# A pass's activations in two halves of two tiles, with ScalarE's two copies of the transposes put before and behind the second activation

## The chip, the cores and the metric

The kernel runs on one core of one Trainium2 chip. The metric is the device time of one execution in microseconds (us), taken as the median of the runs. The engines are named as the profile names them: PE is TensorE's matmul side (PEld its weight loads), ACT is ScalarE, DVE is VectorE, POOL is GpSimd, SP is SyncE, which here only issues DMAs.

## The reference

The computation is one layer of a graph network on 12,500 nodes with 256 channels, all in float32. It normalises x, adds a graph convolution over 200,000 sorted edges and a linear attention, and then a feed-forward part of 30 iterations. The change is in the last one:

```python
def step(h, _):
    h = h + 0.01 * jnp.tanh(h)
    h = h * jax.nn.sigmoid(h)
    h = _layernorm(h, ln_w, ln_b)
    h = jnp.einsum('bsc,dc->bsd', h, W) + b
    return (h, None)
x, _ = jax.lax.scan(step, x, None, length=N_ITERS)     # N_ITERS = 30
```

In front of it stand `x = x + gnn(...) + mix(...)` and a layer norm; behind it the result is added to x.

## The kernel before

**Tiles and groups.** The 12,500 nodes are 98 tiles of 128 rows (the last one partly filled). Four tiles make a group: 24 groups of four tiles and one group of two. A *pass* is one iteration of the feed-forward for one group, so there are 25 x 30 = 750 passes, 720 of them of four tiles.

**Two parts.** Up to about 480 us the kernel normalises x, makes the transposed copies and the attention's matrices, and begins the edge sums. After that one loop (L1083) runs over the *steps* that a planner (`plan`) wrote down beforehand. A step holds at most one item: a pass of a group, or a product for a group's base ("mix" for the attention, "W" for the graph convolution). Up to five groups are under way at a time, and the same group comes again after four steps at the earliest, usually five. Beside the items a step can hold edge work ("octets"): gathers on POOL, selections on DVE (L213, L218, L226), edge matmuls on PE (L239, L261), a copy on ACT (L250 or L275) and a memset on DVE (L276).

**One pass, over several steps.** If a pass is the item of step k:

- Step k, PE: eight transposes of the normed tiles z into two PSUM tiles `pt`, two tiles of nodes each (L1057; four transposes per `pt`). ACT copies each `pt` into its half of `zT` (L1064, two copies of 128x512).
- Step k+1, PE: the product with the weight matrix, 16 matmul instructions (L1070), into a PSUM tile `po` of 128x1024. There are two `po` and two `pt` buffers.
- Step k+2, ACT: `s = tanh(po)` (L1016). DVE: `s = 0.01*s + po` (L1022, called the sum here; it is also the last reader of `po`). ACT: `s = silu(s)` (L1023). DVE: the statistics of s (L1029, two instructions). POOL: the variance and its power -1/2 (L1033, L1035).
- One or two steps later, DVE: z from s and the statistics (L1043, four instructions), and then the transposes of the group's next pass.

So in one step k three passes are at work: the transposes and copies of the pass of step k, the product of the pass of step k-1, and the activations of the pass of step k-2. Every engine takes its instructions in the order in which the loop writes them:

- PE: transposes(k), product(k-1), edge matmuls;
- ACT: edge copy, tanh(k-2), copy 0 (k), copy 1 (k), silu(k-2);
- DVE: selections, memset, sum(k-2), z for the items of the next two steps, statistics(k-2).

The transposes of step k+1 write the same two `pt` buffers that the copies of step k read: the first four wait for copy 0, the last four for copy 1, and product(k), which reads `zT`, stands behind them on PE.

A group's first pass has its own entry ("fresh", L1149 to L1207): statistics of the base, a scaling on ACT and DVE (L1174, L1178), and the same tanh, sum and silu, called from the same functions `act1` and `act2`.

Of the kernel before, what the change touches and what calls it, by code (L numbers as in the profile page):

```python
# [10 lines left out]
AF = mybir.ActivationFunctionType  # L11
ALU = mybir.AluOpType
# [19 lines left out]
def gps_layer(  # L32
# [22 lines left out]
    nc = tc.nc  # L55
# [25 lines left out]
    def rows_io(ap, tl, t0, nt, load, eng):  # L81
        full = nt if (t0 + nt) * P <= N else nt - 1
        parts = []
        if full:
            parts.append((tl[:, :full, :], ap[t0 * P : (t0 + full) * P, :].rearrange("(g p) c -> p g c", p=P)))
        if full < nt:
            parts.append((tl[:TAIL, full, :], ap[(t0 + full) * P : N, :]))
        for s, d in parts:
            if load:
                eng.dma_start(out=s, in_=d)  # L90
            else:
                eng.dma_start(out=d, in_=s)
# [533 lines left out]
    with tc.If(n_out > 0):  # L626
        with ExitStack() as pg_:
# [12 lines left out]
            for t in range(NE):  # L640
# [34 lines left out]
                    op1=ALU.mult, accum_out=cnt[:rows],  # L675
# [22 lines left out]
            for gi, (t0, nt) in enumerate(groups):  # L698
                ac = gp.tile([P, G, C], F32, name="ac", bufs=1)
                load_rows(acc, ac, t0, nt, nc.sync)  # L700
                for j in range(nt):
                    pt = p_t.tile([P, KC, P], F32, name="pt")
# [304 lines left out]

    def flat(h, nt):  # L1010
        return h[:, : nt // 2].rearrange("p q c j -> p (q c j)")

    def act1(gi, h):
        nt = groups[gi][1]
        s = hp.tile([P, G // 2, C, 2], F32, name="s")
        nc.scalar.activation(flat(s, nt), flat(h, nt), AF.Tanh)  # L1016
        return s

    def act2(gi, h, s):
        nt = groups[gi][1]  # L1020
        sf = flat(s, nt)
        nc.vector.scalar_tensor_tensor(sf, sf, 0.01, flat(h, nt), op0=ALU.mult, op1=ALU.add)  # L1022
        nc.scalar.activation(sf, sf, AF.Silu)  # L1023

    def stats(gi, s):
        t0, nt = groups[gi]
# [31 lines left out]
            pts.append(pt)  # L1058
        zTs[gi] = (zT, pts)

    def copies(gi):
        zT, pts = zTs[gi]
        for q, pt in enumerate(pts):
            nc.scalar.activation(zT[:, 2 * q : 2 * q + 2], pt, AF.Copy, bias=1.0)  # L1064

    def matrix(nt, lhsT, rhs, paired=False):
# [16 lines left out]
    for k in range(K + 3):  # L1083
# [5 lines left out]
        kind, gi = item(k)[:2]  # L1089
        if kind in ("mix", "W"):  # L1090
            t0, nt = groups[gi]
# [25 lines left out]
        last = kind2 == "pass" and item(k - 2)[2] == FFN_ITERS - 1  # L1117
        if kind2 == "pass" and not last:
            s2 = act1(g2, pos[kind2, g2])
        if kind == "pass":  # L1120
            copies(gi)
        if kind2 == "pass" and not last:
            act2(g2, pos.pop((kind2, g2)), s2)
        elif last:
            t0, nt = groups[g2]
            for q in range(nt // 2):
                h = pos[kind2, g2][:, q].rearrange("p c j -> p j c")
                r = slice(2 * q, 2 * q + 2)
                nc.vector.tensor_tensor(base[g2][:, r, :], h, base[g2][:, r, :], ALU.add)  # L1129
            pos.pop((kind2, g2))  # L1130
            rows_io(out, base[g2], t0, nt, False, nc.sync)
            written[g2] = k
        elif kind2 == "mix":
            nt = groups[g2][1]
            nc.vector.tensor_tensor(base[g2], pos.pop((kind2, g2))[:, :nt, :], xts.pop((kind2, g2))[:, :nt, :], ALU.add)
            if g2 < ed.weighted:
                aT = ed.aT.pop(g2).rearrange("p k (g n) -> p k g n", n=P)
                for i in range(KC):
                    bk = base[g2][:, :, i * P : (i + 1) * P]
                    nc.vector.scalar_tensor_tensor(bk, aT[:, i], 0.0, bk, op0=ALU.max, op1=ALU.add)  # L1140
        elif kind2 == "W":
            nt = groups[g2][1]
            ac = xts.pop((kind2, g2))[:, :nt, :]
            nc.vector.tensor_tensor(ac, pos.pop((kind2, g2))[:, :nt, :], ac, ALU.add)
            nc.vector.scalar_tensor_tensor(base[g2], ac, 0.0, base[g2], op0=ALU.max, op1=ALU.add)
# [3 lines left out]
        for g3, k3 in fresh:  # L1149
            if k == k3 + 4:  # L1150
                act2(g3, *first_norm[g3])
# [4 lines left out]
        for g3, k3 in fresh:  # L1156
            nt = groups[g3][1]
            if k in (k3 + 2, k3 + 3):
                mv, rs = first_norm[g3, "stats"]
                if k == k3 + 2:  # L1160

                    if 0 in written and written[0] + 2 <= k:
                        h = base[0].rearrange("p g c -> p (g c)").rearrange("p (q c j) -> p q c j", c=C, j=2)
                    else:
                        h = fp.tile([P, G // 2, C, 2], F32, name="z", bufs=3)
                    sh = fp.tile([P, G], F32, name="f_ve")
                    nc.vector.scalar_tensor_tensor(
                        sh[:, :nt], mv[:, :nt, 0], -1.0, rs[:, :nt], op0=ALU.mult, op1=ALU.mult
                    )
                    first_norm[g3, "h"] = (h, sh)  # L1170
                h, sh = first_norm[g3, "h"]
                q = k - k3 - 2
                if 2 * q < nt:
                    nc.scalar.activation(  # L1174
                        h[:, q, :, 0], base[g3][:, 2 * q, :], AF.Identity, bias=sh[:, 2 * q : 2 * q + 1],
                        scale=rs[:, 2 * q : 2 * q + 1],
                    )
                    nc.vector.tensor_scalar(  # L1178
                        h[:, q, :, 1], base[g3][:, 2 * q + 1, :], mv[:, 2 * q + 1, 0:1], rs[:, 2 * q + 1 : 2 * q + 2],
                        ALU.subtract, ALU.mult,  # L1180
                    )
                if k == k3 + 3:
                    first_norm[g3] = (h, act1(g3, h))
# [5 lines left out]
        for g3, k3 in list(fresh):  # L1189
            nt = groups[g3][1]  # L1190
# [48 lines left out]
```

## Time and profile before

| what | value |
|---|---|
| runs of the kernel | 4190.81 us median of 3 (4182.11 to 4192.11) |
| the profiled execution's own time | 4187.49 us |
| its span in the trace | 4185.7 us (1.8 us lie around it) |
| granted clock of TensorE | 0.991 of full speed over the span, 1.00 from 480 us on |
| busy share of the span, PE / DVE / ACT / POOL | 97% / 81% / 60% / 62% |
| loop from 480 to 4186 us: PE / DVE / ACT busy | 3655.6 / 3121.8 / 2344.3 of 3706 us |

How to read it: a row of the profile's groups names the line, the engine and the operation, what is written and read, the shape and the count, then the busy time in us, the mean of one in ns, and after the second bar the time for which the engine stood idle just before such instructions, with what ended it. A row of the timeline gives the start and the length in us, the engine, the line, the operation, the count of instructions merged into the row, and in brackets the idle time of the engine before the row. A busy share is a mean over stages; the end of a matmul is modelled, so that PE's spacing from start to start tells more than its busy time.

### The profile page before, as it was taken

The numbers are of one execution on the slowest core, as the hardware profiler recorded it, in microseconds if no ns is written. First come the engines' busy times: TensorE is split into PE (matmuls) and PEld (weight loads), VectorE is DVE, ScalarE is ACT, GpSimd is POOL, SyncE is SP. The second block draws the span as 40 slices with busy tenths as digits, with TensorE's granted clock in tenths as the row PEclk, the third lists the DMA queues.
The fourth block names the chain that finished last, engine by engine and source line by source line (L and its number), as shares of the span: only waits on it lengthen the run. The fifth ranks groups of instructions, "written<-read, shape, count | busy, mean of one in ns | idle before, by whom it ended". The sixth has DMA issues, their size and how long they took to land.

```text
span 4185.7 us, 67249 instructions
## 1 busy us (share of the span) xinstructions
PE 4057.6 (97%) x23817; PEld 3358.3 (80%) x23817; DVE 3401.4 (81%) x7400; ACT 2523.0 (60%) x3762; POOL 2577.9 (62%) x3189
## 2 busy tenths in 40 slices
PE   8897899999999999999999999999999999999999
PEld 5444678888888888888888888888888888888888
DVE  8554568888888888888888888888888888888887
ACT  7331246666666666666666666666656666667775
POOL 3564666777777777777777777777667652222222
PEclk9898999999999999999999999999999999999999
DMA  8332532222222222222222222222222210000000
GB/s 262 108 87 72 147 98 66 65 61 65 75 61 72 76 64 74 73 66 71 72 65 72 77 65 72 70 74 61 72 70 59 65 50 14 6 6 1 1 1 23
DMA packets 147685, 278.31 MB, mean 66 GB/s; under 512 B 28048, under 2 KB 97198, under 8 KB 147342
## 3 DMA queue, kind: packets, MB, share of 16 engines
q0 software_dynamic: 75024, 204.97, 17.0%
q1 hardware_dynamic: 72173, 68.42, 5.4%
q8 instruction: 194, 3.18, 0.3%
q14 instruction: 150, 1.22, 0.1%
q10 hardware_dynamic: 144, 0.52, 0.0%
HBM read 247.68 MB, written 26.12 MB: 65 GB/s over the span
## 4 chain that ended last, share of the span: by engine, by line
PE 77%; DVE 11%; ACT 3%; issue 3%; POOL 2%; another core or an unknown queue 1%; POOLq 0%; DVEq 0%; ACTq 0%
PE po L1070 53%; PE pt L1057 13%; PE pq L239 4%; DVE z L1043 4%; PE pkv L290 3%; PE pa L261 3%; DVE st L1029 2%; DVE s L1022 2%; ACT s L1016 2%; POOL rs L1035 1%; PE pacc L316 1%; ACT s L1023 1%; POOL xg L187 0%; DVE big L1129 0%
## 5 line engine op out<-in xcount | busy, mean ns | idle before, releaser
L1070 PE MATMUL po<-w,zT 128*128 128x256 f32 x11760 | 2669.8, 380 | 4.8 <-ACT zT L1064 2.3
L1070 PEld LDWEIGHTS po<-w,zT 128*128 128x128 f32 x11760 | 2178.4, 190 | 285.2 <-issue 7.8
L187 POOL DMA_INDIRECT xg<-xnd,src_i x1563 | 1597.4, 1022 | 512.9 <-issue 308.6
L1023 ACT ACTIVATE s<-s 128x1024 f32<-128x1024 f32 (+1 forms) x750 | 780.5, 1041 | 598.5 <-DVE s L1022 584.9
L1043 DVE TENSOR_SCALAR z<-s,st,rs 128x256 f32<-128x256 f32 x2940 | 1031.5, 418 | 100.7 <-POOL rs L1035 96.0
L1029 DVE BATCH_NORM_STATS2 st<-s 128x6 f32<-128x512 f32 x1470 | 938.7, 680 | 181.6 <-ACT s L1023 163.8
L1022 DVE SCALAR_TENSOR_TENSOR s<-s,po 128x1024 f32<-128x1024 f32 x725 | 864.3, 1192 | 251.4 <-ACT s L1016 181.3
L1016 ACT ACTIVATE s<-po 128x1024 f32<-128x1024 f32 x725 | 729.6, 1006 | 209.0 <-PE po L1070 197.6
L1064 ACT ACTIVATE zT<-pt 128x512 f32<-128x512 f32 x1470 | 801.5, 602 | 61.2 <-PE pt L1057 55.0
L1057 PE MATMUL pt<-ident,z 128*128 128x128 f32 x5880 | 792.7, 276 | 38.9 <-DVE z L1043 37.5
L1057 PEld LDWEIGHTS pt<-ident,z 128*128 128x128 f32 x5880 | 670.1, 141 | 182.6 <-issue 81.6
L1035 POOL TENSOR_TENSOR rs<-ve,mhalf 128x4 f32<-128x4 f32 (+1 forms) x750 | 763.3, 1018 | 62.5
L1033 POOL TENSOR_SCALAR ve<-st 128x4 f32<-128x4 f32 (+1 forms) x750 | 147.3, 196 | 933.6 <-DVE st L1029 889.0
L250 ACT COPY sq<-pq 128x256 f32<-128x256 f32 x196 | 72.4, 369 | 284.3 <-PE pq L239 198.2
L239 PE MATMUL pq<-xg,sel 128*32 128x256 f32 x3126 | 222.9, 386 | 8.5 <-issue 6.4
L290 PE MATMUL pkv<-wkv,big 128*128 128x512 f32 x392 | 201.3, 634 | 9.3 <-DVEq L626 4.9
L239 PEld LDWEIGHTS pq<-xg,sel 128*32 128x32 f32 x3126 | 84.7, 109 | 112.1 <-issue 69.5
L261 PE MATMUL pa<-selq,sq 128*128 128x192 f32 (+1 forms) x784 | 163.4, 331 | 9.3 <-ACT sq L250 3.6
L275 ACT COPY aT<-pa 128x128 f32<-128x128 f32 x196 | 51.4, 262 | 194.1 <-PE pa L261 145.6
L261 PEld LDWEIGHTS pa<-selq,sq 128*128 128x128 f32 (+1 forms) x784 | 137.9, 192 | 22.0 <-ACT sq L250 4.7
L301 DVE TENSOR_REDUCE v<-sq 128x8 f32<-128x512 f32 x98 | 66.7, 680 | 92.4 <-ACT sq L297 78.4
L297 ACT ACTIVATE sq<-pkv 128x512 f32<-128x512 f32 x98 | 57.9, 591 | 115.3 <-PE pkv L290 69.1
(163 smaller groups left out, 1553.2 us busy)
## 6 DMA issues: line engine op xcount, KB each, us to landing
xg<-xnd,src_i POOLq DMA_INDIRECT x1563
xt<-in_x_dram SPq DMA_DIRECT2D x48, 512.0 KB
xnd<-xt SPq DMA_DIRECT2D x24, 512.0 KB
out_dram<-big SPq DMA_DIRECT2D x24, 512.0 KB
xt<-accw SPq DMA_DIRECT2D x22, 512.0 KB
ac<-accw SPq DMA_DIRECT2D x2, 512.0 KB
xg<-in_dst_dram SPq DMA_DIRECT2D x6, 128.0 KB
xg<-in_src_dram SPq DMA_DIRECT2D x6, 128.0 KB
```

Of the source, the lines that this page charges most:

```text
L187: nc.gpsimd.indirect_dma_start(out=ed.xg[t], out_offset=None, in_=xnd, in_offset=bass.IndirectOffsetOnAxis(ap=src_i[:, t : t + 1], axis=0),)
L239: nc.tensor.matmul(ed.pq[j * 2 * WIN : (j + 1) * 2 * WIN, :], lhsT=sel[:, j, :], rhs=ed.xg.pop(q * Q + j), start=(q % 2 == 0), stop=last, ...
L261: nc.tensor.matmul(pa[:, k, :], lhsT=sq[:rows, k * P : (k + 1) * P], rhs=selq[:rows, :], start=False, stop=(o == NO - 1), skip_group_check ...
L1016: nc.scalar.activation(flat(s, nt), flat(h, nt), AF.Tanh)
L1022: nc.vector.scalar_tensor_tensor(sf, sf, 0.01, flat(h, nt), op0=ALU.mult, op1=ALU.add)
L1023: nc.scalar.activation(sf, sf, AF.Silu)
L1029: nc.vector.bn_stats(st[:, q, :], s[:, q].rearrange("p c j -> p (c j)"))
L1035: nc.gpsimd.tensor_tensor(rs[:, :nt], ve[:, :nt], mhalf[:, :nt], ALU.pow)
L1043: nc.vector.tensor_scalar(z[:, j, :], s[:, j // 2, :, j % 2], sv[:, j, 1:2], rs[:, j : j + 1], ALU.subtract, ALU.mult)
L1057: nc.tensor.transpose(pt[:, i, k, :], z[:, 2 * q + i, k * P : (k + 1) * P], ident)
L1064: nc.scalar.activation(zT[:, 2 * q : 2 * q + 2], pt, AF.Copy, bias=1.0)
L1070: nc.tensor.matmul(po[:, j // 2, :, j % 2] if paired else po[:, j, :], lhsT=lhsT(j, k), rhs=rhs[:, k, :], start=(k == 0 and (j % 2 == 0 or ...
```

## The change

The functions `act1` and `act2` work on each pair of tiles by itself: two tanh of 128x512 in place of one of 128x1024, then sum and silu of the first pair, sum and silu of the second. The group of two tiles has one pair and keeps its single instructions. `copies` takes the number of the half; copy 0 stands ahead of the sums and silus, copy 1 behind them. Line numbers after this point grow: the tanh is L1018, the sum L1024, the silu L1025, the transposes L1059, the copies L1066 and the product L1072.

```diff
-    def flat(h, nt):
-        return h[:, : nt // 2].rearrange("p q c j -> p (q c j)")
+
+    def parts(t, nt):
+        return [t[:, q].rearrange("p c j -> p (c j)") for q in range(nt // 2)]
 
     def act1(gi, h):
         nt = groups[gi][1]
         s = hp.tile([P, G // 2, C, 2], F32, name="s")
-        nc.scalar.activation(flat(s, nt), flat(h, nt), AF.Tanh)
+        for sf, hf in zip(parts(s, nt), parts(h, nt)):
+            nc.scalar.activation(sf, hf, AF.Tanh)
         return s
 
     def act2(gi, h, s):
         nt = groups[gi][1]
-        sf = flat(s, nt)
-        nc.vector.scalar_tensor_tensor(sf, sf, 0.01, flat(h, nt), op0=ALU.mult, op1=ALU.add)
-        nc.scalar.activation(sf, sf, AF.Silu)
+        for sf, hf in zip(parts(s, nt), parts(h, nt)):
+            nc.vector.scalar_tensor_tensor(sf, sf, 0.01, hf, op0=ALU.mult, op1=ALU.add)
+            nc.scalar.activation(sf, sf, AF.Silu)
...
-    def copies(gi):
+    def copies(gi, half):
         zT, pts = zTs[gi]
-        for q, pt in enumerate(pts):
+        for q, pt in list(enumerate(pts))[half : half + 1]:
             nc.scalar.activation(zT[:, 2 * q : 2 * q + 2], pt, AF.Copy, bias=1.0)
...
         if kind2 == "pass" and not last:
             s2 = act1(g2, pos[kind2, g2])
         if kind == "pass":
-            copies(gi)
+            copies(gi, 0)
         if kind2 == "pass" and not last:
             act2(g2, pos.pop((kind2, g2)), s2)
-        elif last:
+        if kind == "pass":
+            copies(gi, 1)
+        if last:
```

In the built program the order of PE, POOL and SP is the one before. On ACT a step reads: edge copy, tanh, tanh, copy 0, silu, silu, copy 1. On DVE: selections, memset, sum, sum, z, statistics. The waits are these: the first tanh waits for the whole product, and only the second tanh of a pair raises ACT's semaphore (by two), so the first sum waits for both halves; each silu waits for its own sum, each statistics instruction for its own silu, and the last four transposes of the next step for copy 1.

## The prediction

> **What bounds the kernel now.** I read the page's busy shares and groups first, then the waits of PE from 480 us on (the loop), then timelines of single steps.
>
> ```profile
> PE 4057.6 (97%) x23817; PEld 3358.3 (80%) x23817; DVE 3401.4 (81%) x7400; ACT 2523.0 (60%) x3762; POOL 2577.9 (62%) x3189
> L1057 PE MATMUL pt<-ident,z 128*128 128x128 f32 x5880 | 792.7, 276 | 38.9 <-DVE z L1043 37.5
> L1023 ACT ACTIVATE s<-s 128x1024 f32<-128x1024 f32 (+1 forms) x750 | 780.5, 1041 | 598.5 <-DVE s L1022 584.9
> ```
>
> ```profile
> PE pt L1057 <- DVE z L1043: 37.5, 41, 2.4
> ...
> PE po L1070 <- ACT zT L1064: 2.3, 2, 1.5
> ```
>
> PE sets the end. In the loop it is busy for 3655.6 of 3706 us, so no change off PE can win more than the 50 us that are left. Most of them are 41 waits for z (37.5 us); for ACT's copies PE waits twice (2.3 us). ACT's silu, however, waits 584.9 us for the sum. Before, that wait is harmless: nothing that PE needs soon stands behind the silu. **After, copy 1 stands behind it.**
>
> An ordinary step of four tiles takes PE 16 x 0.216 + 8 x 0.109 = 4.33 us (start-to-start distances of back-to-back matmuls and transposes in the trace's records); edge work adds about 1.1 or 0.8 us to some steps.
>
> **Prices of the halves.** The trace has them already, from the group of two tiles and from other 128x512 work:
>
> ```profile
> L1064 ACT ACTIVATE zT<-pt 128x512 f32<-128x512 f32 x1470 | 801.5, 602 | 61.2 <-PE pt L1057 55.0 <-PE po L1070 2.3 <-remote 1.5
> ...
> L1022 DVE SCALAR_TENSOR_TENSOR s<-s,po 128x512 f32<-128x512 f32 x29 | 19.5, 672 | 1.9 <-ACT s L1016 1.9
> ...
> L1023 ACT ACTIVATE s<-s 128x512 f32<-128x512 f32 x30 | 18.9, 629 | 21.9 <-DVE s L1022 21.9
> ```
>
> Two copies in a row take 1.08 to 1.10 us (timeline), so two of 0.60 overlap by 0.11; a pair of tanh halves (0.58 alone) costs about 1.09 against 1.02 whole. Two DVE reads of 128x512 from PSUM in a row (L1129) take 1.28; a pair of sums costs 1.28 against 1.22. A silu half frees ACT after 0.63 - 0.11 = 0.52. The busy sums: 720 x 0.07 = 50 us of ACT, 720 x 0.06 = 43 us of DVE, about as much again of ACT for the silus. DVE goes from 84% to 85% of the loop, ACT from 63% to 66%. Neither becomes the bound by that.
>
> The Trainium skill, "Perfetto Trace Analysis", section "Optimizing Scalar/DVE Operations", gives an overhead per instruction of about 125 ns for DVE on PSUM, 51 ns for ScalarE on PSUM and 93 ns on SBUF, and advises larger operations if the engine is saturated; by it DVE would pay 720 x 0.125 = 90 us (an estimate from that page), twice what the trace's pairs show. The same section says that breaking instructions up may help where these engines are not saturated but cause bubbles elsewhere, which speaks for this change; whether it holds hangs on what waits for what.
>
> **What the split shortens.** Both sums wait for the second tanh, so they start about 0.07 us later than now, not half a tanh earlier. The first silu can run beside the second sum, and the second silu ends 0.03 + 0.63 after its sum, against 0.03 + 1.06 for a whole one: some 0.3 us earlier. But the statistics, which wait for it, stand on DVE behind four z (1.4 us), which start when the sum ends; DVE waits for the silu there in 155 cases only. So z comes earlier in few steps.
>
> **What copy 1 now waits for.** Counted from tanh's start: 1.09 tanh pair, 0.05 to the first sum, 1.28 sums, 0.03 to the second silu, 0.52, copy 0.59, and 0.15 until PE's transpose starts (z's end to transpose start is 0.147 at each of PE's waits for z): 3.71 us. PE needs it at the fifth transpose of the next step, 4.57 us after tanh's start at the median. So there is some 0.9 us to spare as long as the sum starts right after tanh. When DVE is late, they are gone. A step with selections:
>
> ```profile
> 2002.94 1.03 ACT L1016 ACTIVATE s<-po 128x1024 f32<-128x1024 f32 x1
> 2003.86 1.10 ACT L1064 ACTIVATE zT<-pt 128x512 f32<-128x512 f32 x2
> ...
> 2005.66 1.21 DVE L1022 SCALAR_TENSOR_TENSOR s<-s,po 128x1024 f32<-128x1024 f32 x1
> ...
> 2006.90 1.06 ACT L1023 ACTIVATE s<-s 128x1024 f32<-128x1024 f32 x1 [1.95 <-DVE s L1022]
> 2006.91 1.04 PE L1057 MATMUL pt<-ident,z 128*128 128x128 f32 x8
> ```
>
> Tanh is done at 2003.97, but DVE (statistics, selections, memset) comes to the sum at 2005.66. Now both copies are out by 2004.96. After: 2005.66 + 1.28 + 0.03 + 0.52 + 0.59 + 0.15 = 2008.23, and the fifth transpose is due at 2006.91 + 4 x 0.109 = 2007.35. **PE waits 0.88 us**, with the product of this step and all later work behind it. The end of the loop, without edge work, has another such place: after each pass of the two-tile group PE's step is short.
>
> ```profile
> 3805.26 1.02 ACT L1016 ACTIVATE s<-po 128x1024 f32<-128x1024 f32 x1 [0.53 <-PE po L1070]
> 3805.93 1.89 PE L1070 MATMUL po<-w,zT 128*128 128x256 f32 x8
> ...
> 3807.66 1.04 PE L1057 MATMUL pt<-ident,z 128*128 128x128 f32 x8
> ```
>
> 3805.26 + 3.71 = 3808.97 against a need at 3807.66 + 0.44 = 3808.10: 0.87 us late, once in each round of about 15.3 us, and PE's own product starts that tanh, so it comes back every round.
>
> I did this sum for all 661 steps of the trace that have both two copies and a silu, with the later of the old start of the sum and tanh's start + 1.14. (Where the activations are the two-tile group's, their own lengths; where the step's own product comes before the next transposes, its ninth matmul is the need.) 524 are in time; 43 are late by under 0.3 us (5.5 us together), 60 by 0.3 to 1 us (45.7), 34 by more, up to 2.2 (52.4). **Sum 103.6 us**: 3.8 until 1000 us, 26.7 until 2000, 30.0 until 3000, 17.5 until 3740, 25.6 to the end. PE has no slack to take it back from, so it adds to the span except where PE would have waited anyway: at most 23 us of the present waits for z lie within 25 us behind a late copy. Against this, z of a starting group comes later. At 2372 to 2381 us the chain to z runs through ACT and DVE without a pause: two tanh, two sums, one silu, and after the change one copy more; 2 x 0.07 + 2 x 0.06 + 0.59, less 0.4 for the shorter end of the silu, is +0.45, for some 20 of the 41 waits +9 us. Net 103.6 - 23 + 9 = +90.
>
> Two edits cost nothing of their own: copy 0 behind the pair of tanh instead of one (+0.07, due only at the next step's first transpose, 2.5 us later at the median), and `if last` for `elif last`, which issues the same. SP's and POOL's queues keep their order. PE's own wait for `po` (the sum) is covered by the wait for copy 1.
>
> **Rivals.**
>
> *A: the lateness is mostly absorbed.* One DVE backlog makes one late step and PE's pause lets DVE catch up; only the big ones (52.4) remain, less 23: +29, 4216. For it: most late steps stand alone. Against: the rounds at the end are paced by PE and repeat. Between A and the forecast lies about +55.
>
> *B: faster.* The second silu's 0.3 to 0.4 us earlier end passes through the statistics to z and shortens PE's 41 waits: 41 x 0.4 = -16 us, 4171; all of them gone would be -37.5. It decides if the late copies together cost less than 16 us, so if fewer than some 20 of the 137 late steps are late. For it: the wait of the statistics for silu, 163.8 us in 155 cases. Against: DVE's order, and the octet step above.
>
> *C: worse than summed.* The lateness feeds on: ACT ends each step with a copy, so the next tanh starts up to 0.2 us later, DVE's 0.06 per step lengthens its backlogs, and the 52 steps that have under 0.2 us to spare join the 137 late ones. 189 x 0.2 = at most +38, nothing absorbed: 103.6 + 9 + 38 = +151, 4338. Long waits cost more: after the wait of 2.51 us before 2689.09 the product took 5.28 us instead of 3.62 (about 1.7 us more in the records). The Trainium skill, "TensorE: Matmul & The Clock Gate", section "What's actually happening", sets the idle window for the halved clock at about 3.4 us, by which no wait here would cost anything extra; the trace has one at 2.51.
>
> *D: no change.* The waits as I read them are not met on the chip, and gains and losses cancel.
>
> **How the numbers follow.** The profiled execution took 4187.49 us (span 4185.7 and 1.8 around it), 0.08% under the median of the runs, 4190.81; I sum against the former. Forecast +90: **4278 us**. Chances: forecast 0.56, A 0.20, C 0.13, B 0.06, D 0.05. The range from A to C leaves out some 2 in 10: 4216 to 4338. About 0.3% (13 us) is what a measurement of this kernel tells from no change; faster 0.06, same 0.05, slower 0.89.
>
> **What would show it.** Right: the transposes (L1059) wait for copies or for silu on ACT, about 140 times and 70 to 110 us, in the fifth of eight; a stretch of the last 400 us has one such wait of 0.8 us per 15 us; DVE busy up by about 45 us; ACT's wait for sums stays. Wrong: PE's waits still name z only, or the wait for z falls by more than 15 us. If the fifth transpose waits for less than 50 times, the lateness was absorbed (A); if DVE's pairs of sums take over 1.35 us, the price was too low.

## The result, and the profile after

The changed kernel takes **4258.35 us** (median of 4 runs, 4253.8 to 4263.16) against 4187.83 us in the runs beside it: ratio 1.0167, 95% interval 1.0153 to 1.0182, so 70.5 us slower. The profiled execution took 4261.3 us with a span of 4259.4 us, 73.7 us over the span of before. The page after, its busy line and two of its groups:

```profile
PE 4062.7 (95%) x23817; PEld 3356.9 (79%) x23817; DVE 3442.8 (81%) x8120; ACT 2682.0 (63%) x5202; POOL 2572.7 (60%) x3189
...
L1024 DVE SCALAR_TENSOR_TENSOR s<-s,po 128x512 f32<-128x512 f32 x1421 | 909.0, 680 | 450.8 <-ACT s L1018 394.7 <-issue 44.0 <-PE pt L1059 10.8
...
L1059 PE MATMUL pt<-ident,z 128*128 128x128 f32 x5880 | 809.0, 276 | 99.8 <-ACT zT L1066 63.3 <-DVE z L1045 27.5 <-ACT s L1025 6.1
```

The idle time of PE ahead of the transposes rose from 38.9 to 99.8 us, and its first cause is no longer z but `zT`, that is ACT's copy. Before, no wait for ACT is listed in this row. DVE works 41.4 us more, ACT 159.0 us more; PE itself works as before. The waits of PE in the loop, from 480 us on, say the same (us in total, times, longest):

```profile
PE pt L1059 <- ACT zT L1066: 63.3, 78, 1.9
PE pt L1059 <- DVE z L1045: 27.5, 30, 2.7
PE pt L1059 <- ACT s L1025: 6.1, 8, 1.2
```

Here is the step with selections whose timeline the prediction showed, in the changed kernel (rows without edge work, z and statistics):

```profile
2030.26 1.10 ACT L1018 ACTIVATE s<-po 128x512 f32<-128x512 f32 x2
...
2032.88 1.26 DVE L1024 SCALAR_TENSOR_TENSOR s<-s,po 128x512 f32<-128x512 f32 x2
2033.59 1.22 ACT L1025 ACTIVATE s<-s 128x512 f32<-128x512 f32 x2 [1.74 <-DVE s L1024]
...
2034.22 0.60 PE L1059 MATMUL pt<-ident,z 128*128 128x128 f32 x4
...
2034.72 0.58 ACT L1066 ACTIVATE zT<-pt 128x512 f32<-128x512 f32 x1
...
2035.35 0.66 PE L1059 MATMUL pt<-ident,z 128*128 128x128 f32 x4 [0.53 <-ACT zT L1066]
```

The eight transposes have become a row of four and a row of four. DVE comes to the sums 1.5 us after tanh, ACT begins copy 1 only at 2034.72, when PE's first four transposes are already under way, and the fifth starts at 2035.35 instead of 2034.66 (2034.22 + 4 x 0.109): 0.69 us late, where 0.88 was worked out. The place at the end of the loop:

```profile
3856.70 1.04 PE L1059 MATMUL pt<-ident,z 128*128 128x128 f32 x8
...
3858.15 1.27 DVE L1024 SCALAR_TENSOR_TENSOR s<-s,po 128x512 f32<-128x512 f32 x2
...
3859.31 0.60 PE L1059 MATMUL pt<-ident,z 128*128 128x128 f32 x4
...
3859.99 0.58 ACT L1066 ACTIVATE zT<-pt 128x512 f32<-128x512 f32 x1
...
3860.62 0.66 PE L1059 MATMUL pt<-ident,z 128*128 128x128 f32 x4 [0.71 <-ACT zT L1066]
```

3860.62 - 3859.31 - 0.44 = 0.87 us late, as worked out; in the last 110 passes there are 27 such waits with 23.5 us together.

To size this over the whole loop I take PE's start-to-start distances from the trace's records, less the distance without a wait (0.109 us behind a transpose, 0.216 behind a matmul of the product; behind edge work its own usual distance), and add what is over 0.05 us, by place (the products are those of the passes and of the groups' bases):

| PE's waits in the loop, us | before | changed | difference |
|---|---|---|---|
| first transpose of a pass (z) | 46.0 | 39.3 | -6.7 |
| fifth transpose (copy 1; small waits for z) | 10.7 (73) | 90.1 (144) | +79.4 |
| sixth transpose | 0.1 | 6.8 | +6.7 |
| the products | 19.0 | 14.1 | -4.9 |
| sum | 75.8 | 150.3 | +74.5 |

The sum agrees with the 73.7 us of the spans. (The sixth transpose follows the fifth some 0.05 us later than usual in 112 of the 144 cases in which the fifth has waited.)

### The profile page after: what moved, and what is told of

Read it like the earlier page. It is cut to its first block, busy times and chain, and to the rows that moved or that the text cites. A ratio compares the mean times of both kernels' runs of the same rounds, so it can differ in the third digit from the quotient of the medians.

```text
span 4259.4 us, 69797 instructions
## 1 busy us (share of the span) xinstructions
PE 4062.7 (95%) x23817; PEld 3356.9 (79%) x23817; DVE 3442.8 (81%) x8120; ACT 2682.0 (63%) x5202; POOL 2572.7 (60%) x3189
## 4 chain that ended last, share of the span: by engine, by line
PE 61%; DVE 19%; ACT 8%; issue 5%; POOL 3%; another core or an unknown queue 1%; DMA 0%; POOLq 0%; ACTq 0%; DVEq 0%
PE po L1072 41%; PE pt L1059 10%; DVE z L1045 7%; PE pq L239 4%; DVE st L1031 4%; DVE s L1024 4%; ACT s L1018 3%; ACT s L1025 3%; PE pa L261 2%; PE pkv L290 2%; POOL rs L1037 2%; ACT zT L1066 1%; POOL xg L187 1%; DVE se L213 1%
## 5 line engine op out<-in xcount | busy, mean ns | idle before, releaser
L1072 PE MATMUL po<-w,zT 128*128 128x256 f32 x11760 | 2666.8, 380 | 3.3 <-ACT s L1025 1.5
L1072 PEld LDWEIGHTS po<-w,zT 128*128 128x128 f32 x11760 | 2177.4, 190 | 279.6 <-issue 8.6
L1024 DVE SCALAR_TENSOR_TENSOR s<-s,po 128x512 f32<-128x512 f32 x1421 | 909.0, 680 | 450.8 <-ACT s L1018 394.7
L1025 ACT ACTIVATE s<-s 128x512 f32<-128x512 f32 x1470 | 900.3, 630 | 493.2 <-DVE s L1024 482.0
L1066 ACT ACTIVATE zT<-pt 128x512 f32<-128x512 f32 x1470 | 869.7, 595 | 60.3 <-PE pt L1059 53.3
L1018 ACT ACTIVATE s<-po 128x512 f32<-128x512 f32 x1421 | 773.7, 598 | 209.1 <-PE po L1072 195.8
L1059 PE MATMUL pt<-ident,z 128*128 128x128 f32 x5880 | 809.0, 276 | 99.8 <-ACT zT L1066 63.3
L1059 PEld LDWEIGHTS pt<-ident,z 128*128 128x128 f32 x5880 | 671.2, 141 | 257.8 <-ACT zT L1066 115.5
```

The lines of the kernel that those rows point to most:

```text
L1018: nc.scalar.activation(sf, hf, AF.Tanh)
L1024: nc.vector.scalar_tensor_tensor(sf, sf, 0.01, hf, op0=ALU.mult, op1=ALU.add)
L1059: nc.tensor.transpose(pt[:, i, k, :], z[:, 2 * q + i, k * P : (k + 1) * P], ident)
L1072: nc.tensor.matmul(po[:, j // 2, :, j % 2] if paired else po[:, j, :], lhsT=lhsT(j, k), rhs=rhs[:, k, :], start=(k == 0 and (j % 2 == 0 or ...
```

## The experiments

They ran on three chips: e1 to e4 on chip 1, e5 to e8 on chip 10, e9 and e10 on chip 0. On each of them the kernel before takes 4087 to 4088 us, against 4188 us in the first measurements, for which the record gives no number of a chip. The ratios are to the runs of the kernel before on the same chip; the one trace of that kernel in this set, e7, is of chip 10. **Theory**: PE waits for copy 1 because it stands behind the silus, and so behind DVE's sums. **Rivals**: the halves cost by themselves (more instructions); or they gain, and the copies' place hides it. In the table the waits of PE are summed as above, and the ratio has its 95% interval.

| kernel | copy 1 stands | ratio | z | fifth | products |
|---|---|---|---|---|---|
| e7: before | ahead | 1 | 35.6 | 9.7 | 16.2 |
| e9: the change | behind | 1.0142 (1.0126 to 1.0157) | 28.9 | 79.6 | 7.9 |
| e1: halves | ahead | 0.9975 (0.9965 to 0.9984) | 29.8 | 7.1 | 14.4 |
| e2: no halves | behind | 1.0227 (1.0211 to 1.0242) | 25.7 | 111.2 | 11.7 |
| e3: halves | between the silus | 1.0053 (1.0037 to 1.0068) | 33.3 | 35.9 | 10.1 |
| e4: halves | ahead in 144 passes | 0.9988 (0.9979 to 0.9997) | 32.3 | 9.1 | 16.3 |
| e5: halves, whole tanh | ahead | 0.9971 (0.9961 to 0.9982) | 29.5 | 7.2 | 14.4 |
| e6: halves, product in two tiles | ahead | 0.9911 (0.9896 to 0.9927) | 17.3 | 5.8 | 5.9 |
| e10: as e6 | between the silus | 0.9936 (0.9922 to 0.995) | 16.2 | 17.7 | 4.0 |
| e8: as e6 | behind | 0.9969 (0.9957 to 0.9981) | 13.1 | 33.4 | 3.7 |

**e1, the halves alone.**

```diff
         if kind == "pass":
             copies(gi, 0)
+            copies(gi, 1)
         if kind2 == "pass" and not last:
             act2(g2, pos.pop((kind2, g2)), s2)
-        if kind == "pass":
-            copies(gi, 1)
```

> The halves of the change, but both copies ahead of the silus as in the kernel before. Theory (copy 1 behind the silus makes PE wait at the fifth transpose): these waits fall from 144 with 90 us to about 70 with 11 us as before, and the time comes back to 4188 +-15 us. Rival (the halves themselves cost: 41 us more of DVE and 159 us more of ACT): the time stays over 4225 us with PE's waits spread over z and the product. Rival (the halves gain): under 4175 us, by shorter waits for z.

The loss is gone, and more: 10.8 us faster than before. The waits at the fifth transpose are back, and those for z are 5.8 us shorter:

```profile
PE pt L1059 <- DVE z L1045: 22.5, 28, 1.9
```

The same row in e7, the kernel before:

```profile
PE pt L1057 <- DVE z L1043: 28.2, 33, 2.4
```

So the halves do not cost, in spite of the added busy time, and all of the loss is in the place of copy 1.

**e2, the move alone.** Tanh, sum and silu as before; `copies` and its two calls as in the change.

> The other part alone: whole tanh, sum and silu as before, copy 1 behind the silu. The silu holds ACT for 0.95 us instead of 0.52 after its sum, so by the prediction's sum over the steps 198 of 661 are late, by 159 us together (with the change 137 and 103.6; there 90 were measured). Theory: 4187 + 110 to 150 us, so slower than the change, 4295 to 4340. Rival (the cost comes from the halves): about 4188.

4180.07 us, 92.6 us slower: the move is worse without the halves, as the theory says, but I had expected 110 to 150 us. 152 waits with 111.2 us at the fifth transpose stand against 198 steps with 159 us in the sum. The same view as above:

```profile
PE pt L1057 <- ACT zT L1064: 94.8, 118, 2.3
```

**e3, copy 1 between the silus.** `act2` takes the halves one by one: copy 0, sum and silu of the first pair, copy 1, sum and silu of the second pair.

> The halves, with copy 1 between the two silus: it then waits for the first sum alone, and stands behind one silu half. By the sum over the steps 83 are late by 42.6 us. Theory: a third to a half of the loss stays, 4205 to 4230 us, and the waits at the fifth transpose are 30 to 50 us. Rival (any place behind a sum costs the same): 4250 to 4260. Rival (halves gain once copy 1 is early enough): under 4185.

21.9 us slower than before, with 35.9 us at the fifth transpose: a third of the loss, as worked out. Against e1, which has the halves too, it loses 33 us where the change loses 69 (58.6 in e9 and e1's 10.8). What copy 1 costs grows with what stands ahead of it; no run tells the sums' part from the silus'.

**e4, ahead only where it was late.** The set holds the 144 passes behind which the fifth transpose waited in the changed kernel's trace.

```diff
         if kind == "pass":
+            n_pass += 1
             copies(gi, 0)
+            if n_pass in LATE:
+                copies(gi, 1)
...
-        if kind == "pass":
+        if kind == "pass" and n_pass not in LATE:
             copies(gi, 1)
```

> The change, but in the 144 passes (of 750) whose copy 1 made the fifth transpose wait in the changed kernel's trace, copy 1 is ahead of the silus; in the other passes it stays behind. Theory (only late steps cost, the other copies have slack): nearly all of the 71 us come back, 4180 to 4205 us, with under 25 us of waits at the fifth transpose. Rival (the lateness moves to the next step, since DVE's backlog is the same): half of it stays, 4215 to 4235.

4083.47 us: all of the loss comes back, with 9.1 us at the fifth transpose. The other 576 pairs keep copy 1 behind the silus, and that costs little: e4 is 6.8 us slower than e1, where all stand ahead, and every run of e4 is slower than every run of e1. Most of the lateness did not move on to other steps.

**e5, whole tanh.** As e1, with one tanh of 128x1024.

> As e1_both_ahead (both copies ahead), but with one whole tanh; sums and silus in halves. e1 came out at 0.9975 of the kernel before. Theory: its gain is that of the silu halves alone (the second half ends 0.3 to 0.4 us earlier, statistics and z follow), and the tanh halves only cost 0.07 us a step: ratio 0.995 to 0.998. Rival (the tanh halves won it): 0.999 to 1.002.

The same as e1 (4076.87 and 4076.66 us). The halves of tanh show neither gain nor cost here; e1's gain is that of the sums and silus. That fits what the built program shows: the first sum waits for both tanh.

**e7 and e9, before and the change again, beside the experiments.**

> The kernel before, unchanged, for a trace of this chip: ratio 1.00, waits of PE for z about 46 us and at the fifth transpose about 11 us in the loop, as in its first trace. If the waits for z are 30 us here, e1's 30 us were no gain.

> The change itself, unchanged, on the chip of the experiments (whose first 390 us run faster): if its loss is that of the late copies in the loop, it is the same in us, ratio 1.015 to 1.021, with 85 to 95 us of waits at the fifth transpose. If it hung on the slower start of the first chip, it is under 1.010.

The change loses 58.6 us here against 70.5 at first, with 79.6 us at the fifth transpose against 90.1; both are just below what I had expected. The first pass begins at 391.7 us in e7 and at 473.9 us in the first trace of the same kernel, so most of the 98 us between the two traces lie ahead of the loop, and the greater part of the loss does not hang on them. Waits for z are 35.6 us here, so 29.8 in e1 was a gain of 6, not of 16.

**e6, e8 and e10, halves that overlap.** The product goes into two tiles of 128x512 instead of one of 128x1024:

```diff
-    p_o = ph.enter_context(tc.tile_pool(name="pf_o", bufs=2, space=PSUM))
+    p_o = ph.enter_context(tc.tile_pool(name="pf_o", bufs=4, space=PSUM))
...
-        po = p_o.tile([P, G // 2, C, 2] if paired else [P, G, C], F32, name="po")
+        po = [p_o.tile([P, C, 2] if paired else [P, 2, C], F32, name="po") for _ in range(nt // 2)]
```

The base additions, which read `po` too, become two instructions. In the built program the first tanh then waits for the product's first eight matmul instructions only, and the first sum for the first tanh only.

> As e1_both_ahead, but the product's output is two tiles of 128x512 with four buffers in place of one of 128x1024 with two, so that the first tanh waits for the first half of the product alone and the first sum for the first tanh alone. Theory (PE is bound, some 50 us of its waits are left): 5 to 25 us better than e1, ratio 0.991 to 0.997. Rival (DVE's order holds z back whatever ACT does): the same as e1, 0.997 to 0.999.

4052.88 us: 35.5 us faster than before, and the best version of this study. Waits for z halve to 17.3 us; in PE's list:

```profile
PE pt L1060 <- DVE z L1046: 11.1, 18, 1.9
```

A rival is that the four smaller buffers come free sooner. It can explain only a few of the 24 us to e1: there PE waits 0.6 us for a sum that still reads `po`, and its weight loads 3.8 us.

> The change (copy 1 behind the silus) with the product in two tiles as in e6. Theory (late steps come from DVE's backlog ahead of the sum): by the sum over the steps of the trace of before 131 steps are still late by 92 us (with the change 137 by 104), so most of the loss stays: ratio 1.009 to 1.016. Rival (late steps come from the sum's wait for the second tanh): the loss is gone, under 1.004.

This expectation fell. With the change's order of the copies the kernel is now 12.9 us faster than before, and waits at the fifth transpose are 33.4 us in 69 cases instead of 92 in 131. I had kept DVE's earlier work where it was. But by the traces DVE was late in good part because its own sums had waited for tanh. That wait, in the change (e9, the first row) and in e8 (the second):

```profile
DVE s L1024 <- ACT s L1018: 417.7, 346, 3.1
```

```profile
DVE s L1025 <- ACT s L1019: 267.3, 330, 3.4
```

The same place at the end of the loop as above, in e8:

```profile
3692.05 0.60 ACT L1019 ACTIVATE s<-po 128x512 f32<-128x512 f32 x1
3692.74 1.27 DVE L1032 BATCH_NORM_STATS2 st<-s 128x6 f32<-128x512 f32 x2
3693.57 1.04 PE L1060 MATMUL pt<-ident,z 128*128 128x128 f32 x8
3693.77 0.60 ACT L1019 ACTIVATE s<-po 128x512 f32<-128x512 f32 x1 [1.13 <-PE po L1073]
3693.94 1.26 DVE L1025 SCALAR_TENSOR_TENSOR s<-s,po 128x512 f32<-128x512 f32 x2
...
3695.80 0.59 ACT L1067 ACTIVATE zT<-pt 128x512 f32<-128x512 f32 x1
3696.18 1.04 PE L1060 MATMUL pt<-ident,z 128*128 128x128 f32 x8
```

The first tanh runs 1.5 us before the step's transposes (3693.57), the statistics of the pass before begin 0.8 us ahead of them, and the sums 0.4 us behind them. In the changed kernel the same sums began at 3858.15, 1.45 us behind the transposes at 3856.70. Copy 1 ends at 3696.39; with the 0.15 us of the hand-over that is 0.08 us before the fifth transpose of the next step is due (3696.18 + 0.44), and the eight transposes run as one row again.

> The product in two tiles as in e6, copy 1 between the two silus. Ahead of them gave 0.9911, behind them 0.9969 with 33 us of waits at the fifth transpose. If the place of copy 1 is paid by the sums that it waits for, one sum instead of two: 0.991 to 0.994, with 8 to 18 us of these waits. If what matters is only that copy 1 is not last: 0.991, and if any place behind a sum costs the same: 0.996.

0.9936, between its neighbours, with 17.7 us at the fifth transpose: the first sum that copy 1 waits for costs 12 us of these waits, the second 16 more (e6, e10, e8: 5.8, 17.7, 33.4 us).

## Why the prediction was right, point by point

- **The mechanism and the time.** +90 us were forecast, +70.5 measured (+73.7 between the profiled executions). The fifth transpose waits 144 times (73 before, of 0.15 us on average), against about 140 forecast; e1, e2 and e4 show the place of copy 1 to be the whole loss.
- **The prices of the halves** hold: a tanh pair takes 1.09 us at the median, a pair of sums 1.28, and from the end of the sums to the end of copy 1 it is 1.16 us in the step with selections (2034.14 to 2035.30) against 1.14. DVE's added 41.4 us were forecast as 43. ACT's 159 us were undersized (about 100): the silus' group rose by 120 us, and the copies' by 68, for which nothing had been put, since two copies that stand apart no longer overlap. It cost nothing, since ACT has room.
- **The sum over the steps** is the term that was mis-sized. 103.6 us in 137 steps were forecast; the waits at the fifth transpose rose by 79.4, from 10.7 to 90.1, so 24 us less. 109 of the 137 steps are among the 144. In the 60 steps of 0.3 to 1 us 38.8 us were measured for 45.7, in the 34 over 1 us 40.1 for 52.4. A likely reason is rival A's, that DVE works on while PE waits and later backlogs are smaller; no run separates it, and 24 us are far less than the 51 that A supposed. The sixth transpose's 6.7 us, which the sum did not have, made up for a part by luck.
- **What comes back.** I took off 23 us of waits for z and added 9 for late starts of groups, net -14; measured were -6.7 for z and -4.9 for the products.
- **The end of the loop**: 0.87 us a round was forecast and met to 0.01 us; 25.6 us from 3740 us on, against 23.5 in the last 110 passes.
- **Rival B** was a real effect, at the size given: taken by themselves (e1, e5) the halves gain 11 us, where 16 were named; of PE's waits 5.8 us less are for z, 2.6 at the fifth transpose and 1.8 at the products (e1 against e7). That could not show beside 79 us of waits.
- **Rival C**: DVE's wait for tanh went from 181.3 to 394.7 us, which fits a later start of the next tanh; but it rises with both copies ahead too, from 231.3 (e7) to 331.4 (e1). PE did not lose more than the sum by it.
- **The Trainium skill**, "Perfetto Trace Analysis", section "Optimizing Scalar/DVE Operations": by an estimate from its overhead of about 125 ns for a DVE instruction on PSUM the 720 further ones would have made 90 us; DVE's busy time rose by 41.4, 58 ns each, and the measurement decides. The advice to break instructions up where they cause bubbles elsewhere came true in e6 and, with 11 us, in e1, where the first tanh hands nothing on before the second is done; in the change the place of copy 1 costs more than that.
- **Rival C's note that long waits cost more** can be read in the trace of before, in two waits for z of the same length:

```profile
3562.59 1.31 PE L1057 MATMUL pt<-ident,z 128*128 128x128 f32 x8 [2.35 <-DVE z L1043]
3563.74 5.31 PE L1070 MATMUL po<-w,zT 128*128 128x256 f32 x16
...
3637.18 1.31 PE L1057 MATMUL pt<-ident,z 128*128 128x128 f32 x8 [2.36 <-DVE z L1043]
3638.33 3.62 PE L1070 MATMUL po<-w,zT 128*128 128x256 f32 x16
```

Behind the first the granted clock is half for 3.41 us (matmuls 0.427 us apart), behind the second it is not. In e7 a wait of 1.92 us has such a stretch behind it, at 2284.4 us; in the changed kernel, of 15 waits of 1.6 to 2.9 us ahead of the last pass, only the longest has. So neither the note nor the window that it quotes tells which wait costs more, and the measurement decides: the changed kernel has one such stretch in the loop ahead of its last pass where before had two, so the loss is not this.

- **The ceiling of 50 us** that the prediction put on all gains was read from PE's busy time, whose ends are modelled. By the spacing of starts PE's waits were 75.8 us. The forecast does not use it.

What stays open: why the 28 forecast steps without a wait (9.1 us) were in time, step by step, and why the loop of the same kernel has fewer waits for z in e7 than in the first trace (35.6 against 46.0 us).

## What to carry to other kernels

Work that a bound engine needs soon must not be queued behind work that waits for a slower neighbour: add up, from the trace, the way from that neighbour's start to the moved instruction's end, and hold it against the time at which the bound engine comes to it, step by step; a mean hides it, since 576 of 720 steps here had room. Splitting an operation paid here where the first half was handed on: see what the first half waits for and who may start on it, and split the buffers (here the product's) along with the instructions. When a sum over steps is made from an old trace, remember that the engine called late may itself have been waiting for what is being changed.

## What the runs showed that was not expected

The same kernel, with the same mean clock of 1.00 in the loop, took 4187.49 us in the first trace and 4089.46 us in e7; its first pass began at 473.9 and 391.7 us, so 82 of the 98 us lie in the first part, which the change does not touch. What makes that part slower in the first trace stays open. And after a wait at the fifth transpose the sixth mostly comes some 0.05 us later than usual too (late in 120 cases in all, 6.8 us).
